# Bank reads first, tiles half a pair apart, and a fixed TensorE order in the second pass of a two-layer graph kernel

## The chip, the cores and the metric

The kernel runs on one NeuronCore of one Trainium2 chip. The metric is the device time of one execution in microseconds (us). The kernel before takes 2579.47 us, the median of three runs that lie between 2577.24 and 2579.74 us. The profiled execution spans 2577.0 us; every time that is read from the trace counts from its start.

Five engines run beside each other, each with a queue of its own: TensorE (PE in the profile; its weight loads are shown apart as PEld), VectorE (DVE), ScalarE (ACT), GpSimd (POOL) and the DMA-issuing SyncE (SP).

## The reference

There are 128 graphs of 64 nodes with 768 features. Two layers of a graph network run one after the other. Only the second one is touched here:

```python
def _L1_gnn_ref(feat_in, adj, W, b, w_src, w_dst, H_w, H_b):
    h = jnp.einsum('bni,hio->bhno', feat_in, W)          # 6 heads of 128
    th = jnp.tanh(h)
    attn_src = jnp.einsum('bhno,hoz->bhnz', th, w_src)
    attn_dst = jnp.einsum('bhno,hoz->bhnz', th, w_dst)
    attn = attn_src + jnp.swapaxes(attn_dst, -1, -2)
    attn = jnp.where(attn >= 0, attn, leaky_alpha * attn)
    attn = jnp.where((adj == 0)[:, None, :, :], NEG_MASK, attn)
    attn = jax.nn.softmax(attn, axis=-1)
    feat_out = jnp.einsum('bhnm,bhmo->bhno', attn, h) + b
    feat_out = jax.nn.elu(...)                           # heads side by side: 768 columns
    gate = jax.nn.sigmoid(feat_in @ H_w.T + H_b)
    return gate * feat_out + (1.0 - gate) * feat_in

x = x + _L0_gnn_ref(relu(layernorm(x)), ...)             # pass 1 of the kernel
x = x + _L1_gnn_ref(relu(layernorm(x)), ...)             # pass 2 of the kernel
```

So each row of 768 features is multiplied by two 768 x 768 matrices (`W`, all heads, and `H_w`), and a small attention inside each graph of 64 nodes follows.

## The kernel before

Two graphs make a tile of 128 rows, and two tiles (`t0`, `t1`) make a pair; there are 32 pairs. Pass 2 multiplies the 256 rows of a pair by both matrices at once with a bilinear scheme of 15 products of blocks in place of 18. `f...` are sums of transposed blocks of the input, `g...` and `b...` sums of weight blocks, and each product is added in one of four PSUM banks a, b, c and d. After each product VectorE (and, where an output block begins, ScalarE too) reads the bank and adds it to an output block of the tile.

```python
PRODUCTS = (      # A side, B side, bank, bank starts anew, output block (tile, third), sign, ...
    ("f1", "g6", "a", True, "11", "+", False),
    ("f7", "g10", "b", True, "00", "-", False),
    ("a01", "b11", "d", True, "01", "+", True),
    ("f4", "b21", "a", False, "01", "-", False),
    ("a00", "g12", "b", False, "01", "-", False),
    ("f3", "g8", "c", True, "12", "-", False),
    ("a02", "g14", "a", False, "00", "-", False),
    ("f9", "g9", "b", False, "02", "+", False),
    ("f11", "b10", "d", True, "00", "+", True),
    ("f6", "g5", "a", False, "02", "+", False),
    ("f8", "g3", "b", False, "12", "-", False),
    ("f10", "b12", "c", False, "02", "+", True),
    ("f5", "b22", "a", False, "12", "-", False),
    ("a11", "g1", "b", False, "11", "+", True),
    ("f2", "g11", "a", False, "10", "+", True),
)
```

`P1` to `P15` below are these products in this order. The code of pass 2, cut to what the change and the steps of the prediction touch:

```python
psm = px.enter_context(tc.tile_pool(name="psm1", bufs=2, space=bass.MemoryType.PSUM))
pss = px.enter_context(tc.tile_pool(name="pss1", bufs=2, space=bass.MemoryType.PSUM))  # two buffers "ps"

def merged(main, side):              # writes the side steps between the numbered main steps
    side = sorted(side, key=lambda e: e[0])
    ...
def turn(p, k, q):                   # transposes two blocks of the next pair's input   (L704)
    ps = pss.tile([P, 512], F32, name="ps")...
    for i in range(KQ):
        nc.tensor.transpose(ps[:, i, :], H1[2 * p + k][...], ident)
    a = OPS[p, f"a{k}{q}"] = ...
    nc.scalar.copy(a, ps)                                                  # (L709)

def read(b, c, sign, first, ss):     # after a product
    ...
    op = nc.vector.tensor_add if sign == "+" else nc.vector.tensor_sub
    if not first:
        ... op(to, ps, to) or op(to, to, ps)                               # (L736, L738)
        return
    if ss.start == 0:
        nc.scalar.activation(to[:, 0], ps[:, 0], AF.Copy, ...)             # (L741)
    if ss.stop == 2:
        ... op(to[:, s], ps[:, s], hbb[:, cols])                           # (L746, L748)

def product(an, bn, b, first, c, sign, begins, ss):
    def step(q):                     # two steps (q = 0, 1) a product
        if first and q == 0:
            bank[b] = psm.tile([P, 512], F32, name=f"pm{b}", bufs=2 if b == "a" else 1)
        nc.tensor.matmul(bank[b][...], OPS[p, an][:, q, :], bw2[bn][...], ...)   # (L755)
        if q == KQ - 1:
            read(b, c, sign, begins, ss)

def heads(t):                        # tanh, products with w_src and w_dst, sums by head
    th = work.tile([P, H, DO], F32, name="th")
    nc.scalar.activation(th, HS[t], AF.Tanh)                               # (L774)
    pr = work.tile([P, 2, H, DO], F32, name="pr")
    nc.vector.tensor_mul(pr, th..., wsd...)                                # (L776)
    for h in range(H):               # 12 activations with an accumulator  (L781, L783)
        nc.scalar.activation(pr[:, 1, h, :], pr[:, 1, h, :], AF.Copy, accum_out=sd[:, 1, h : h + 1])
    ...                              # then a short chain on GpSimd into sdb (L784 to L791)

def rows(t):                         # (L803): PE, then DVE into rrow (L805) and ACT into lrow (L807)
    ps = pss.tile([P, 512], F32, name="ps")
    nc.tensor.matmul(ps[:NR, : N + P], sdb[t % 2]..., idr, start=True, stop=True)
    ...
def gate(t):
    nc.scalar.activation(Z[t], Z[t], AF.Tanh, scale=0.5)                   # (L811)

def softmax(t):
    pl = pss.tile([P, 512], F32, name="ps")...
    nc.tensor.matmul(pl, lrow[t % 2], rrow[t % 2], start=True, stop=True)  # (L819)
    nc.vector.copy_predicated(a, AI[p]..., pl)                             # (L821)
    nc.scalar.activation(al, a, AF.Prelu, alpha=LEAKY)                     # (L823)
    nc.vector.tensor_reduce(mx, al, AX.X, OP.max, negate=True)             # (L825)
    for h in range(H):                                                     # six exponentials (L829)
        nc.scalar.activation(pb[:, h, :], al[:, h, :], AF.Exp, bias=mx[:, h : h + 1],
                             accum_out=dn[:, h : h + 1])
    nc.vector.reciprocal(dn, dn)

def turn_p(t):                       # three transposes of the probabilities (L840), two heads in each
    ps = pss.tile([P, 512], F32, name="ps")...
    for c in range(HH):
        nc.tensor.transpose(ps[:, c, :], PB[t][:, 2 * c : 2 * c + 2, :]..., ident)
    nc.scalar.copy(pt, ps)                                                 # (L842)

def attend(t):                       # 12 small matmuls (L857), then six reads by VectorE (L861)
    po = [pss.tile([P, 512], F32, name="ps")... for r in range(2)]
    ...
def final(t, c0=0, c1=D):            # ACT exponential (L871), three DVE operations (L872 to L874), out
    ...
```

`before(p)` transposes the next pair's blocks, `own(p)` forms sums and calls `heads(t0)`, `behind(p)` holds the rest of the attention of the pair before. Nothing in the source fixes the order on an engine: a scheduler takes the instructions of all engines and orders each engine's queue by priority (earlier in the source first) as its own model finds them ready. What is fixed in the built program is that each engine takes its queue in that order.

Of the kernel before, what the change touches and what calls it, by code (L numbers as in the profile page):

```python
# [8 lines left out]
F32 = mybir.dt.float32  # L9
# [70 lines left out]
def kernel(  # L80
# [558 lines left out]
    with ExitStack() as px:  # L639
# [78 lines left out]
        def main(p):  # L718
# [2 lines left out]
            steps = []  # L721
            for k in range(2):
                t = 2 * p + k
                HS[t] = hzs[t % 4][:, 0, :].rearrange("p (h o) -> p h o", h=H)
                Z[t] = hzs[t % 4][:, 1, :]

            def read(b, c, sign, first, ss):

                k, q = int(c[0]), int(c[1])
                cols = slice(q * CQ, (q + 1) * CQ)  # L730
                to = hzs[(2 * p + k) % 4][:, ss, cols]
                ps = bank[b][:, : (ss.stop - ss.start) * CQ].rearrange("p (s n) -> p s n", n=CQ)
                op = nc.vector.tensor_add if sign == "+" else nc.vector.tensor_sub
                if not first:
                    if sign == "+":
                        op(to, ps, to)  # L736
                    else:
                        op(to, to, ps)  # L738
                    return
                if ss.start == 0:  # L740
                    nc.scalar.activation(to[:, 0], ps[:, 0], AF.Copy,  # L741
                                         scale=1.0 if sign == "+" else -1.0)
                if ss.stop == 2:
                    s = 1 - ss.start
                    if sign == "+":
                        op(to[:, s], ps[:, s], hbb[:, cols])  # L746
                    else:
                        op(to[:, s], hbb[:, cols], ps[:, s])  # L748

            def product(an, bn, b, first, c, sign, begins, ss):  # L750
                def step(q):
                    if first and q == 0:
                        bank[b] = psm.tile([P, 512], F32, name=f"pm{b}", bufs=2 if b == "a" else 1)
                    n = ss.stop - ss.start
                    nc.tensor.matmul(  # L755
                        bank[b][:, : n * CQ], OPS[p, an][:, q, :],
                        bw2[bn][:, (2 * q + ss.start) * CQ : (2 * q + ss.stop) * CQ],
                        start=(first and q == 0), stop=(q == KQ - 1), skip_group_check=True)
# [159 lines left out]

        def last():


            p = NP - 1
            t0, t1 = 2 * p, 2 * p + 1
            return [(31, lambda: (heads(t1), swap(t1))),
                    (31, lambda: load_x(t0)),
                    (33, lambda: load_x(t1)),
                    (38, lambda: rows(t0)),
                    (40, lambda: softmax(t0)),
                    (46, lambda: rows(t1)),
                    (48, lambda: softmax(t1)),  # L930
                    (54, lambda: turn_p(t0)),
                    (56, lambda: attend(t0)),
                    (99, lambda: gate(t0)),
                    (99, lambda: gate(t1)),
                    (99, lambda: turn_p(t1)),
# [58 lines left out]
```

## Time and profile before

| | |
|---|---|
| device time, median of 3 | 2579.47 us |
| span of the profiled execution | 2577.0 us |
| PE busy | 2489.3 us (97%) |
| DVE busy | 1980.3 us (77%) |
| ACT busy | 1079.5 us (42%) |
| first transpose of pass 2 on PE | 1513.72 us |
| first product of the last pair | 2513.76 us |
| last matmul of the attention | 2562.4 us |

"PE" counts the matmul records; "PEld" counts the weight loads, which run beside matmuls. In a list of instructions in order of time each row has a start, a duration, the engine, the line of the source, what is written from what, and how often; a bracket at the end of a row tells how long the engine stood idle before it and which instruction ended the wait. A product of two matmuls of 128 x 512 shows as four records of line 755.

### The profile page before, as it was taken

To read this page: it belongs to the slowest core of one execution; us is meant where nothing else is said; L and a number is where in the kernel's file an instruction comes from. 1 tells how busy PE (TensorE), PEld (TensorE's weight loads), DVE (VectorE), ACT (ScalarE), POOL (GpSimd) and SP (SyncE) were. 2 spreads that over 40 slices of the span, in tenths; PEclk is the share of its full clock that TensorE was granted. 3 is DMA by queue.
4 is the path that set the end of the run, shared out by engine and by line. 5 is a ranking of instruction groups with operands and counts; after the bars stand their busy time and mean duration, and the time that the engine had idled before them with its cause. 6 is when DMAs were issued, how large, how long until landed. Compare 5 with 4: busy or idle time off the path is not lost.

```text
span 2577.0 us, 35545 instructions
## 1 busy us (share of the span) xinstructions
PE 2489.3 (97%) x12072; PEld 1714.2 (67%) x12072; DVE 1980.3 (77%) x4130; ACT 1079.5 (42%) x3588; POOL 492.3 (19%) x801
## 2 busy tenths in 40 slices
PE   5999999999999999999999999999999999999996
PEld 4788888888888888888888864444444444444444
DVE  8977777777777777777777557888888888888887
ACT  1222222222222122222222216666666666666666
POOL 0121121211212112121121111222222222222222
PEclk8999999999999999999999999999999999999998
DMA  5122121221312212122121263444444444444433
GB/s 172 56 74 80 52 102 52 76 78 52 103 52 76 78 52 102 52 78 76 52 101 50 79 203 78 100 100 100 99 100 100 101 100 101 99 100 100 100 75 77
DMA packets 115047, 224.19 MB, mean 87 GB/s; under 512 B 36538, under 2 KB 48941, under 8 KB 114866
## 3 DMA queue, kind: packets, MB, share of 16 engines
q1 hardware_dynamic: 105208, 196.70, 23.3%
q0 software_dynamic: 9504, 25.17, 6.9%
q8 instruction: 95, 1.56, 0.3%
q14 instruction: 86, 0.70, 0.1%
q10 hardware_dynamic: 154, 0.06, 0.0%
HBM read 95.67 MB, written 100.66 MB: 76 GB/s over the span
## 4 chain that ended last, share of the span: by engine, by line
PE 71%; DVE 18%; ACT 6%; issue 4%; DMA 1%; POOL 1%; SPq 0%; POOLq 0%; DVEq 0%; ACTq 0%
PE pwa L544 19%; PE pwb L544 16%; PE pwc L544 6%; PE pma L755 6%; PE pwd L544 6%; PE pmb L755 6%; PE pb L497 5%; DVE f L861 3%; ACT pb L829 3%; DVE op L243 3%; PE pmc L755 2%; DVE pr L776 2%; DVE f L874 2%; DVE f L872 2%; DVE weights L738 1%
## 5 line engine op out<-in xcount | busy, mean ns | idle before, releaser
L544 PE MATMUL pwa<-weights,op 128*128 128x256 f32 x2304 | 542.6, 383 | 4.3 <-DVE x L536 3.1
L544 PEld LDWEIGHTS pwa<-weights,op 128*128 128x128 f32 x2304 | 423.0, 190 | 73.4 <-DVE x L536 12.0
L243 DVE TENSOR_TENSOR op<-op 128x768 f32<-128x768 f32 (+1 forms) x512 | 339.8, 683 | 156.4 <-ACT op L505 154.5
L505 ACT COPY op<-pb 128x768 f32<-128x768 f32 x160 | 124.2, 798 | 757.0 <-PE pb L497 757.0
L755 PE MATMUL pma<-weights,op 128*128 128x512 f32 (+1 forms) x792 | 381.5, 597 | 35.2 <-DVE weights L738 29.3
L544 PE MATMUL pwb<-weights,op 128*128 128x256 f32 x1536 | 372.2, 383 | 12.9 <-DVE x L538 9.5
L544 PEld LDWEIGHTS pwb<-weights,op 128*128 128x128 f32 x1536 | 285.9, 191 | 60.7 <-DVE x L538 10.3
L755 PE MATMUL pmb<-weights,op 128*128 128x512 f32 (+1 forms) x528 | 252.4, 591 | 3.6 <-DVE weights L738 3.5
L755 PEld LDWEIGHTS pma<-weights,op 128*128 128x128 f32 x792 | 137.8, 191 | 173.8 <-issue 96.4
L225 POOL TENSOR_TENSOR rn<-ve,mhalf 128x1 f32<-128x1 f32 x128 | 89.0, 695 | 530.5 <-DVE ve L224 526.9
L544 PE MATMUL pwc<-weights,op 128*128 128x256 f32 x768 | 184.9, 383 | 0.0
L544 PE MATMUL pwd<-weights,op 128*128 128x256 f32 x768 | 176.2, 379 | 0.0
L755 PEld LDWEIGHTS pmb<-weights,op 128*128 128x128 f32 x528 | 97.0, 193 | 118.4 <-issue 82.9
L218 DVE BATCH_NORM_STATS2 st<-x 128x6 f32<-128x384 f32 x256 | 136.4, 547 | 44.7 <-DMA x<-in_x_dram 43.5
L476 POOL COPY c<-cnt 128x243 bf16<-128x243 bf16 x64 | 46.2, 751 | 649.3 <-PE pb L484 602.3
L497 PE MATMUL pb<-r,h 64*128 64x192 f32 x1536 | 153.0, 339 | 7.8 <-ACT h L406 7.7
L544 PEld LDWEIGHTS pwc<-weights,op 128*128 128x128 f32 x768 | 143.2, 190 | 25.1 <-issue 7.0
L544 PEld LDWEIGHTS pwd<-weights,op 128*128 128x128 f32 x768 | 145.9, 190 | 19.8
L572 ACT ACTIVATE hf<-x,rn 128x768 f32<-128x768 f32 x64 | 65.8, 1028 | 213.7 <-DVE rn L226 213.7
L497 PEld LDWEIGHTS pb<-r,h 64*128 64x128 f32 x1536 | 124.6, 189 | 42.7 <-issue 30.5
L829 ACT ACTIVATE pb<-al,mx 128x64 f32<-128x64 f32 x384 | 128.3, 335 | 14.8 <-DVE mx L825 14.8
L574 POOL TENSOR_TENSOR x<-x,hf 128x768 f32<-128x768 f32 x64 | 115.9, 1812 | 85.4 <-ACT hf L572 85.4
(152 smaller groups left out, 4160.3 us busy)
## 6 DMA issues: line engine op xcount, KB each, us to landing
x<-in_x_dram SPq DMA_DIRECT2D x64, 384.0 KB
h<-hf SPq DMA_DIRECT2D x64, 384.0 KB
out_dram<-x SPq DMA_DIRECT2D x64, 384.0 KB
hh<-hh SPq DMA_DIRECT2D x64, 384.0 KB
h<-h SPq DMA_DIRECT2D x64, 384.0 KB
x<-hh SPq DMA_DIRECT2D x64, 384.0 KB
hx<-weights SPq DMA_DIRECT2D x128, 192.0 KB
out_dram<-f POOLq DMA_DIRECT2D x62, 384.0 KB, 4.9
```

The source lines that it names most:

```text
L218: ins = nc.vector.bn_stats(st[:, i, :], src[:, i * HALF : (i + 1) * HALF])
L225: nc.gpsimd.tensor_tensor(to[:, 0:1], ve, mhalf, op=OP.pow)
L243: return (nc.vector.tensor_add if s1 == "+" else nc.vector.tensor_sub)(to, x, y)
L497: nc.tensor.matmul(ps[:, g, i * 3 * N : (i + 1) * 3 * N], H0[t][s, kb * P : (kb + 1) * P], rts[p % 2][s, k].rearrange("p s n -> p (s n)"), ...
L505: nc.scalar.copy(a.rearrange("p h s (g n) -> p g (h s) n", g=GT), ps[:, :, : 6 * N].rearrange("p g (x n) -> p g x n", n=N))
L544: nc.tensor.matmul(bank[b][:, :CQ], OPS[p, an][:, q, s, :], bw[bn][:, (s * KQ + q) * CQ : (s * KQ + q + 1) * CQ], start=(first and q == s ...
L572: nc.scalar.activation(h, X[t], AF.Relu, scale=to[:, 0:1], bias=to[:, 1:2])
L574: nc.gpsimd.tensor_add(X[t], X[t], h)
L755: nc.tensor.matmul(bank[b][:, : n * CQ], OPS[p, an][:, q, :], bw2[bn][:, (2 * q + ss.start) * CQ : (2 * q + ss.stop) * CQ], start=(first a ...
L776: nc.vector.tensor_mul(pr, th[:, None].to_broadcast([P, 2, H, DO]), wsd.rearrange("p s (h o) -> p s h o", h=H))
L829: nc.scalar.activation(pb[:, h, :], al[:, h, :], AF.Exp, bias=mx[:, h : h + 1], accum_out=dn[:, h : h + 1])
L861: nc.vector.scalar_tensor_tensor(FF[t][:, h * DO : (h + 1) * DO], po[h % 2][:, h // 2, :], DN[t][:, h : h + 1], bb, op0=OP.mult, op1=OP.add)
```

## The change

Pass 1 stays as it is. In pass 2 four things change:

- **Bank reads take precedence.** The reads of a product's bank are put in with a high priority, so the scheduler places them ahead of other work that is ready on VectorE and ScalarE. They are to free a bank as soon as its product is done.
- **The two tiles of a pair run half a pair apart.** The attention of `t0` stays one pair behind; the attention of `t1` starts half a pair later, and its `turn_p`, `attend` and `final` fall two pairs behind (`behind2`). This is to spread the attention work over the pair.
- **Six places for the outputs.** A tile's outputs (`HS`, `Z`) live longer so, and get six places in place of four; the two new ones are tiles of their own. To make room, `pr` has one buffer in place of two.
- **TensorE keeps the written order.** `manual_schedule` for PE takes the order of the PE queue from the source; the four other queues are still ordered by the scheduler.

```diff
+    NHZ = 6
...
+        hzs += [wb.tile([P, 2, D], F32, name=f"hz{i}") for i in range(4, NHZ)]
...
-                HS[t] = hzs[t % 4][:, 0, :].rearrange("p (h o) -> p h o", h=H)
-                Z[t] = hzs[t % 4][:, 1, :]
+                HS[t] = hzs[t % NHZ][:, 0, :].rearrange("p (h o) -> p h o", h=H)
+                Z[t] = hzs[t % NHZ][:, 1, :]
...
                     if q == KQ - 1:
-                        read(b, c, sign, begins, ss)
+                        with tc.high_priority():
+                            read(b, c, sign, begins, ss)
...
-            pr = work.tile([P, 2, H, DO], F32, name="pr")
+            pr = work.tile([P, 2, H, DO], F32, name="pr", bufs=1)
...
         def behind(p):
...
-            return [(0, lambda: gate(t0)),
-                    (1, lambda: (heads(t1), swap(t1))),
-                    (2, lambda: load_x(t0)),
-                    (4, lambda: gate(t1)),
-                    (4, lambda: rows(t0)),
-                    (6, lambda: softmax(t0)),
-                    (10, lambda: load_x(t1)),
-                    (11, lambda: rows(t1)),
-                    (13, lambda: softmax(t1)),
-                    (12, lambda: turn_p(t0)),
-                    (14, lambda: attend(t0)),
-                    (15, lambda: final(t0)),
-                    (19, lambda: turn_p(t1)),
-                    (21, lambda: attend(t1)),
-                    (22, lambda: final(t1))]
+            return [(1, lambda: gate(t0)),
+                    (7, lambda: rows(t0)),
+                    (9, lambda: softmax(t0)),
+                    (9, lambda: (heads(t1), swap(t1))),
+                    (10, lambda: load_x(t0)),
+                    (14, lambda: gate(t1)),
+                    (17, lambda: turn_p(t0)),
+                    (19, lambda: attend(t0)),
+                    (20, lambda: final(t0)),
+                    (22, lambda: rows(t1)),
+                    (24, lambda: softmax(t1)),
+                    (25, lambda: load_x(t1))]
+
+        def behind2(p):
...
+            return [(2, lambda: turn_p(t1)),
+                    (4, lambda: attend(t1)),
+                    (5, lambda: final(t1))]
...
         # last(): the steps of the last pair, moved later and joined by turn_p, attend and
         # final of the tile before (cut)
...
+        px.enter_context(tc.manual_schedule(engines={mybir.EngineType.PE}))
         for _, step in before(0):
             step()
         for p in range(NP):
-            more = [(3, lambda: finish(NP - 1))] if p == 0 else []
+            more = behind(p - 1) + behind2(p - 2)
+            if p == 0:
+                more.append((3, lambda: finish(NP - 1)))
             if p == NP - 1:
-                more += last()
-            merged(main(p), own(p) + before(p + 1) + behind(p - 1) + more)
+                more = [(1.3 * i, f) for i, f in more] + last()
+            merged(main(p), own(p) + before(p + 1) + more)
```

More of the change, by code (lines that the diff above doesn't have):

```diff
@@ L730, in read @@
                 cols = slice(q * CQ, (q + 1) * CQ)
-                to = hzs[(2 * p + k) % 4][:, ss, cols]
+                to = hzs[(2 * p + k) % NHZ][:, ss, cols]
                 ps = bank[b][:, : (ss.stop - ss.start) * CQ].rearrange("p (s n) -> p s n", n=CQ)
@@ L902, in behind @@
             t0, t1 = 2 * p, 2 * p + 1
-            return [(0, lambda: gate(t0)),
-                    (1, lambda: (heads(t1), swap(t1))),
-                    (2, lambda: load_x(t0)),
-                    (4, lambda: gate(t1)),
-                    (4, lambda: rows(t0)),
-                    (6, lambda: softmax(t0)),
-                    (10, lambda: load_x(t1)),
-                    (11, lambda: rows(t1)),
-                    (13, lambda: softmax(t1)),
-                    (12, lambda: turn_p(t0)),
-                    (14, lambda: attend(t0)),
-                    (15, lambda: final(t0)),
-                    (19, lambda: turn_p(t1)),
-                    (21, lambda: attend(t1)),
-                    (22, lambda: final(t1))]
+            return [(1, lambda: gate(t0)),
[11 more added lines that the diff above has]
+        def behind2(p):
+            if p < 0:
+                return []
+            t1 = 2 * p + 1
+            return [(2, lambda: turn_p(t1)),
+                    (4, lambda: attend(t1)),
+                    (5, lambda: final(t1))]
         def last():
@@ L923, in last @@
             t0, t1 = 2 * p, 2 * p + 1
[L924 to L932, printed above, removed]
+            tl = t0 - 1
+            tl = t0 - 1
+            return [(32, lambda: (heads(t1), swap(t1))),
+                    (34, lambda: load_x(t0)),
+                    (36, lambda: load_x(t1)),
+                    (46, lambda: rows(t0)),
+                    (47, lambda: turn_p(tl)),
+                    (49, lambda: softmax(t0)),
+                    (50, lambda: attend(tl)),
+                    (51, lambda: final(tl)),
+                    (54, lambda: rows(t1)),
+                    (57, lambda: softmax(t1)),
+                    (99, lambda: turn_p(t0)),
+                    (99, lambda: attend(t0)),
                     (99, lambda: gate(t0)),
```

## The prediction

> **What bounds the kernel now.** I read the busy shares of the page, then its slices, then the waits of TensorE in pass 2, then one pair in order of time.
>
> ```profile
> span 2577.0 us, 35545 instructions
> PE 2489.3 (97%) x12072; PEld 1714.2 (67%) x12072; DVE 1980.3 (77%) x4130; ACT 1079.5 (42%) x3588; POOL 492.3 (19%) x801
> PE   5999999999999999999999999999999999999996
> ```
>
> TensorE is busy almost throughout. Whatever changes the time must shorten or lengthen its queue. Its waits between 1600 and 2500 us, all of them but one of 0.3 us:
>
> ```profile
> PE pma L755 <- DVE weights L738: 28.5, 28, 1.0
> ```
>
> One wait of 1.0 us in each pair. PE and VectorE in order of time show where, and then ScalarE's durations:
>
> ```profile
> 1934.40 1.88 PE L755 MATMUL pmd<-weights,op 128*128 128x512 f32 x4
> 1937.29 1.13 PE L755 MATMUL pma<-weights,op 128*128 128x512 f32 x2 [1.02 <-DVE weights L738]
> ...
> 1935.35 0.95 DVE L874 SCALAR_TENSOR_TENSOR f<-weights,f 128x768 f32<-128x768 f32 x1
> 1936.22 0.42 DVE L243 TENSOR_TENSOR op<-op 128x256 f32<-128x256 f32 x1
> 1936.56 0.68 DVE L738 TENSOR_TENSOR weights<-weights,pma 128x512 f32<-128x512 f32 x1
> ...
> 1918.02 0.33 ACT L829 ACTIVATE pb<-al,mx 128x64 f32<-128x64 f32 x1
> 1918.35 0.33 ACT L829 ACTIVATE pb<-al,mx 128x64 f32<-128x64 f32 x1
> 1919.88 0.46 ACT L842 COPY pT<-ps 128x384 f32<-128x384 f32 x1
> 1936.64 0.36 ACT L741 ACTIVATE weights<-pma 128x256 f32<-128x256 f32 x1
> 1936.91 0.37 ACT L741 ACTIVATE weights<-pmd 128x256 f32<-128x256 f32 x1
> ```
>
> P15 may not write bank a before P13's read has emptied it, and VectorE does that read only after elementwise work (L874, L243). The product before began at 1934.40 and takes 1.72 us, so PE loses 1937.29 - 1934.40 - 1.72 = 1.17 us. The pair lasts 1937.29 - 1905.04 = 32.25 us, in which the table of stretches gives PE 31.23, DVE 26.57 and ACT 22.51 us of work. So the best that any reordering can bring here is 1.17 us in each of about 30 pairs: 35 us, 1.4%.
>
> **What the Trainium skill says.** "PSUM — Partial Sum Buffer", section "Engine vs sequencer instructions": the queues of ScalarE, VectorE and GpSimdE are strict first-in first-out, and matmuls start and finish in program order. The trace agrees: the 0.68 us read stood 1.2 us behind the elementwise work while PE waited for it. So the order in which a queue was built is the order in which it runs, and a ready instruction behind one that waits does not pass it. "Perfetto Trace Analysis", section "Tensor Engine Instruction (MATMUL, LD_WEIGHTS)": a matmul's end in the profile is estimated. Here a product's records end 0.16 us after the next product starts (1.88 against 1.72), and a ScalarE read starts 0.04 us after that end (1907.02 to 1907.06); I use 0.20 us from a product's nominal end to a reader's start.
>
> **The change, part by part.** No arithmetic is added or removed: a pair still has 15 products, 12 + 6 transposes, 24 attention matmuls. What decides is the order of the queues, which can be read in the built program. It is the same in each of the pairs numbered 2 to 30 (29 pairs) on PE, DVE and ACT; pass 1 is unchanged. On PE around the pair's start it is P15, P1, three transposes of `turn_p(t1)`, P2, `attend(t1)`, P3. ScalarE's order there:
>
> ```
> tanh (heads); gate; Prelu of t1's softmax; 2 accumulations; read of P15; 1 accumulation;
> 4 exponentials of t1; READ OF P1; 2 exponentials of t1; 7 accumulations; READ OF P2;
> 2 accumulations; COPY OF pT (t1); ...
> ```
>
> The bank reads have gone in front of attention work that PE needs *before or right after* the very product they wait for. Four waits follow, each from the start spacing of ScalarE instructions above: a read 0.27, an exponential 0.33, an accumulation 0.29 (L781, 1933.43 to 1933.72), pT 0.47, hand-over to PE 0.08 (pT ends 1920.34, PE starts 1920.42), a transpose 0.11, an input copy 0.25 started, 0.37 whole.
>
> 1. Transposes of `turn_p(t1)`. The last two exponentials run only after the read of P1, and the third transpose needs them: 0.20 + 0.27 + 0.66 + 0.15 (accumulator read and hand-over) = 1.28 us after P1's end, then 0.11 for itself. Unhindered, all three take 0.33. Loss 1.28 + 0.11 - 0.33 = 1.06 us at the least.
> 2. `attend(t1)` needs pT, which stands behind the read of P2 and two accumulations: 0.20 + 0.27 + 0.58 + 0.47 + 0.08 = 1.60 us after P2's end. Nothing stands between P2 and attend on PE. Loss 1.6 us.
> 3. `attend(t0)` now follows four input transposes directly, and there are only two "ps" buffers, so it needs both input copies. They can start 0.42 us after the first transpose (1925.28 to 1925.70) and the second ends at about 1.05; with the hand-over the second attention matmul starts at 1.09, where the transposes end at 0.44. Loss 0.6 us.
> 4. In P12 two pairs of input transposes stand together. The second reuses the "ps" buffer of `rows(t1)`, which ScalarE frees with lrow (0.26 us) queued behind the copy of the first pair: 0.42 + 0.26 + 0.26 + 0.04 = 0.98, where PE would go on at 0.22. Loss 0.76 us.
>
> Sum 4.0 us. Against it stands the wait that goes: the read of P13 now has only one elementwise operation of 0.95 us ahead of it and P14's 1.72 us to run in, so 1.17 us is gained. Net +2.8 us a pair as a floor. I also walked the three queues through one whole pair with these durations. There the exponentials come another 0.2 us late (the max waits behind the 1.68 us product of `heads`, L776), `rows(t0)` waits 0.35 us for VectorE to free its buffer, and `softmax(t0)` waits 0.33 us for lrow, which stands behind the 0.94 us exponential of `final`. That makes 4.9 us of waits, +3.7 net. Small pauses of PE, some 0.1 us after attention matmuls, will swallow part of the last two. I take the middle, +3.3 us: a pair of 35.5 us.
>
> 29 x 3.3 = 96 us. Pair 1 has half of it: +1. In the last pair PE now waits, in the profile before, 2.48 + 3.55 + 0.78 + 1.14 us; the new order puts products into those holes but more attention of the tile before into this pair: -2. Together 2579.5 + 96 + 1 - 2 = 2674 us.
>
> **The rivals.**
>
> *A. The reads win what they aim at.* The 1.17 us wait goes and the attention waits are hidden: 2579 - 35 = 2544, with a tighter last pair perhaps 2535. For it: DVE (26.6) and ACT (22.5) have room in 32 us, and spreading t0 and t1 removes a crowd. Against it: waits 1 and 2 do not depend on how busy ScalarE is, since its queue waits for a product that PE has just finished.
>
> *B. The time stays within 2%.* For this the four losses would have to add up to under 3 us in place of 4 to 4.9, so that less than 1.8 us a pair is left after the gain. One of the two large waits would have to be half as long, by a ScalarE that passes data on faster than the rows above show, or the transposes and attention would have to find other buffers than I read in the build. Against it: the durations come from the same instructions. Then 2590 to 2630.
>
> *C. Worse than the sum.* A late `turn_p` delays everything ScalarE does next (pT, tanh of t1, the product of `heads`, the sums for `rows`), and these come back as a later `rows` and `softmax`, a loop around the pair that I closed with the soft waits of 0.35 and 0.33 only. If it opens further, +5 us a pair: 2725.
>
> **Range and chances.** The floor of the four waits gives 2579 + 29 x 2.8 = 2660, the walk 2579 + 29 x 3.7 = 2687, and either way a few us for the last pair. Widened by a hand-over misjudged by 0.2 us at each of four places (0.8 x 29 = 23 us): 2640 to 2705. The 2% mark lies at 2631, that is +1.8 us a pair; the two large waits alone (2.66 - 1.17 = 1.5) stay below it, and with both small ones they pass it clearly. Faster by over 2% would take 52 us, more than all of PE's waits: 0.02. Within 2% 0.10, slower 0.88.
>
> **What would show it.** In the profile after, PE's waits in pass 2 should name ScalarE: about 1.1 us in each pair for pb (exponentials) before the transposes of `turn_p`, about 1.6 us for pT before attend, 0.6 and 0.76 us for input copies and lrow; the wait for VectorE's read of P13 should be gone; PE's work a pair should stay at 31.2 us and the pair last 35.5. ScalarE should stand idle for a PE product just ahead of those exponentials and of pT. I am wrong if the pair takes 31 to 32 us, or if PE's waits name VectorE or a DMA, or if the loss lies at the end of the kernel rather than in every pair.

## The result, and the profile after

The changed kernel takes 2672.57 us (median of four runs, 2671.89 to 2674.03). The kernel before took 2578.56 us beside it. The ratio is 1.0365, with a 95% interval of 1.0348 to 1.0383: 3.65% slower, 94 us. The prediction said 2674.

The page of the kernel after, its span, busy times and TensorE's slices:

```profile
span 2670.9 us, 35403 instructions
PE 2506.5 (94%) x12072; PEld 1731.6 (65%) x12072; DVE 2009.1 (75%) x4130; ACT 1079.1 (40%) x3588; POOL 487.1 (18%) x801
PE   6999999999999999999999998989899898988995
```

The matmuls are the same 12072, and TensorE's share falls from 97% to 94%. Pass 1 (the nines on the left) is untouched; in pass 2 the nines are now mixed with eights. So most of the time was lost in waits, spread evenly over pass 2. The waits of TensorE between 1600 and 2590 us name them; the columns after the colon are us in total, how often, and the longest:

```profile
PE ps L860 <- ACT pT L845: 39.7, 28, 1.4
PE ps L843 <- ACT pb L832: 25.9, 56, 0.6
PE ps L706 <- ACT op L711: 13.0, 28, 0.5
PE ps L822 <- ACT lrow L810: 7.1, 28, 0.5
PE ps L860 <- ACT op L711: 6.8, 28, 0.2
PE ps L806 <- DVE f L864: 4.6, 28, 0.2
```

Before, there was one wait in each pair, for VectorE's read of P13. It is gone. Six others stand in its place, and five of them name ScalarE: for pT ahead of `attend` (L860), for the exponentials ahead of `turn_p` (L843), for the input copies (L711), for lrow (L810).

The two largest are seen in TensorE's list in order of time. The idle time in brackets is shorter than the loss, since a record runs on for a while after the next instruction could have started (1.88 us for a product that takes 1.72); I read the losses from start to start.

```profile
2000.71 0.27 PE L843 MATMUL ps<-ident,pb 128*128 128x128 f32 x1
2001.31 0.33 PE L843 MATMUL ps<-ident,pb 128*128 128x128 f32 x1 [0.33 <-ACT pb L832]
2002.24 0.33 PE L843 MATMUL ps<-ident,pb 128*128 128x128 f32 x1 [0.60 <-ACT pb L832]
2002.40 1.88 PE L757 MATMUL pmb<-weights,op 128*128 128x512 f32 x4
2005.71 0.32 PE L860 MATMUL ps<-weights,pT 64*64 64x128 f32 x1 [1.42 <-ACT pT L845]
```

The three transposes take 2002.40 - 2000.71 = 1.69 us in place of 0.33. P2 starts at 2002.40, and after its 1.72 us TensorE has nothing to do until pT is there: 2005.71 - 2004.12 = 1.59 us.

ScalarE at the same time (L832 exponentials, L743 bank reads, L786 accumulations, L845 the copy pT), and below it VectorE a little earlier (L779 the product of `heads(t0)`, L828 the max of the softmax of t1, without which no exponential can start):

```profile
2000.83 0.34 ACT L832 ACTIVATE pb<-al,mx 128x64 f32<-128x64 f32 x1
2001.16 0.36 ACT L743 ACTIVATE hz<-pma 128x256 f32<-128x256 f32 x1
2001.42 0.34 ACT L832 ACTIVATE pb<-al,mx 128x64 f32<-128x64 f32 x1
...
2003.83 0.30 ACT L786 ACTIVATE pr<-pr 128x128 f32<-128x128 f32 x1
...
2004.32 0.38 ACT L743 ACTIVATE hz<-pmb 128x256 f32<-128x256 f32 x1
...
2004.90 0.30 ACT L786 ACTIVATE pr<-pr 128x128 f32<-128x128 f32 x1
2005.19 0.47 ACT L845 COPY pT<-ps 128x384 f32<-128x384 f32 x1
...
1996.84 1.74 DVE L779 TENSOR_TENSOR pr<-th,wsd 128x1536 f32<-128x1536 f32 x1
1999.10 0.54 DVE L828 TENSOR_REDUCE mx<-al 128x6 f32<-128x384 f32 x1
```

The read of P1 stands between the fourth and the fifth exponential. The read of P2 starts 0.20 us after P2's end, two accumulations and pT follow. That is the predicted chain. But ScalarE hardly stood idle ahead of either read (no gap ahead of the first, some 0.2 us ahead of the second). From the first exponential on it had work of its own to do almost all the time. And the exponentials started late, only 0.88 us before P1 ended (1999.83 to 2000.71), because the max stood on VectorE behind the 1.74 us product. This matters below.

The last pair, two of TensorE's longest waits there:

```profile
2641.26 0.34 PE L822 MATMUL ps<-rrow,lrow 82*128 82x384 bf16 x1 [2.77 <-ACT lrow L810]
...
2654.86 0.52 PE L843 MATMUL ps<-ident,pb 128*128 128x128 f32 x3 [2.22 <-DVE f L864]
```

Where the 93.9 us between the two profiles lie:

| | before | after | difference |
|---|---|---|---|
| up to the first product of the last pair | 2513.76 us | 2598.66 us | +84.9 |
| last pair and tail | 63.2 us | 72.2 us | +9.0 |
| for comparison: one pair in mid-pass | 32.25 us | 35.27 us | +3.02 |

29 such pairs make +87.6 us; what lies ahead of them gives back 84.9 - 87.6 = -2.7 us.

### The profile page after: what moved, and what is told of

Its sections match the earlier page's. It is cut to its first block, busy times and chain, and to the rows that moved or that the text cites. A ratio compares the mean times of both kernels' runs of the same rounds, so it can differ in the third digit from the quotient of the medians.

```text
span 2670.9 us, 35403 instructions
## 1 busy us (share of the span) xinstructions
PE 2506.5 (94%) x12072; PEld 1731.6 (65%) x12072; DVE 2009.1 (75%) x4130; ACT 1079.1 (40%) x3588; POOL 487.1 (18%) x801
## 4 chain that ended last, share of the span: by engine, by line
PE 75%; ACT 9%; DVE 6%; issue 4%; POOL 3%; DMA 2%; SPq 0%; POOLq 0%; ACTq 0%; DVEq 0%
PE pwa L545 18%; PE pwb L545 15%; PE pwc L545 6%; PE pma L757 6%; PE pmb L757 6%; PE pwd L545 6%; PE pb L498 5%; PE pmc L757 4%; ACT pr L784 3%; ACT pb L832 2%; POOL sdb L792 2%; PE pmd L757 2%; DVE pr L779 2%; PE ps L706 1%; PE ps L860 1%
## 5 line engine op out<-in xcount | busy, mean ns | idle before, releaser
L757 PE MATMUL pma<-weights,op 128*128 128x512 f32 (+1 forms) x792 | 372.7, 586 | 2.3 <-DVE weights L748 1.5
L757 PEld LDWEIGHTS pma<-weights,op 128*128 128x128 f32 x792 | 145.0, 191 | 154.2 <-issue 149.0
L779 DVE TENSOR_TENSOR pr<-th,wsd 128x1536 f32<-128x1536 f32 x64 | 112.0, 1751 | 42.8 <-ACT th L777 42.8
L784 ACT ACTIVATE pr<-pr 128x128 f32<-128x128 f32 x384 | 113.8, 298 | 74.2 <-DVE pr L779 40.5
```

The costliest lines, as they stand in the source:

```text
L757: nc.tensor.matmul(bank[b][:, : n * CQ], OPS[p, an][:, q, :], bw2[bn][:, (2 * q + ss.start) * CQ : (2 * q + ss.stop) * CQ], start=(first a ...
```

## The experiments

The change has three parts that can be set apart: bank reads first, the half-pair distance with its six places, and the fixed order of TensorE. My theory (Q in the expectations) was the prediction's: the reads of P1 and P2, put in front of attention work on ScalarE, make the two large waits. The rival (F): the fixed order is to blame, which lets TensorE do nothing else while it waits. A third (S): the longer distance of t1 and its six places cost.

**e1: after without precedence for the reads.**

```diff
-                        with tc.high_priority():
-                            read(b, c, sign, begins, ss)
+                        read(b, c, sign, begins, ss)
```

> The changed kernel without the high priority of the bank reads; all else stays. Theory Q (ScalarE's queue order: reads that wait for a product stand ahead of attention work that TensorE needs): ScalarE now has all six exponentials ahead of the reads of P15 and P1, and the pT copy ahead of the read of P2, so TensorE's waits for pb (0.9 us a pair) and pT (1.4) go. But VectorE now has the product of heads, the max and a sum ahead of the read of P13, so P15 waits again for VectorE, some 1.8 us. Together about 34.3 us a pair, 2635 to 2655 us. Rival F (the fixed TensorE order is what costs): no change, 2672 within 6 us. Rival S (the longer distance of t1 and six output places cost): no change either.

Measured: 2640.39 us, ratio 1.0232 (1.0215 to 1.0249), a pair of 34.23 us. As expected. The two largest waits of TensorE, 1600 to 2500 us:

```profile
PE pma L757 <- DVE weights L740: 25.8, 17, 1.5
PE pma L757 <- DVE hz L740: 13.7, 9, 1.5
```

These two rows, 26 pairs together, are the wait for P13's read, back again and longer than before, since VectorE's 1.7 us product of `heads` now stands in front of that read too. The waits for pb and pT are gone. Precedence thus costs 32 us here, and the kernel is still 60 us slower than before: two thirds of the loss lie elsewhere.

**e2: after, with `attend(t1)` and `final(t1)` one product later.**

```diff
-                    (4, lambda: attend(t1)),
-                    (5, lambda: final(t1))]
+                    (6, lambda: attend(t1)),
+                    (7, lambda: final(t1))]
```

> The changed kernel with attend(t1) one product later (behind P3 and not behind P2); the read of P2 still stands ahead of the pT copy on ScalarE. Theory Q: pT is ready 1.6 us after P2's end, P3 takes 1.72 us, so the wait for pT goes and nothing else changes: -1.4 to -1.6 us a pair, 33.8 us, 2622 to 2634 us in all. Rival F: the order is as fixed as before, 2672. Rival S: 2672.

Measured: 2705.43 us, ratio 1.048 (1.0464 to 1.0495), pairs of 35.30 and 36.88. A miss, and in the wrong direction. The wait for pT went as expected. The largest wait of TensorE, and then one of its places in TensorE's list and VectorE's:

```profile
PE ps L806 <- DVE f L864: 52.2, 25, 2.1
```

```profile
1983.39 0.25 PE L806 MATMUL ps<-idr,sdb 128*82 128x192 bf16 x1 [2.09 <-DVE f L864]
...
1979.86 1.76 DVE L779 TENSOR_TENSOR pr<-th,wsd 128x1536 f32<-128x1536 f32 x1 [1.27 <-ACT th L777]
...
1981.87 1.64 DVE L864 SCALAR_TENSOR_TENSOR f<-ps,dn,bb 128x128 f32<-128x128 f32 x6
```

`rows(t0)` now comes half a product after `attend(t1)`. It needs a "ps" buffer that `attend` has filled, and VectorE empties it only behind the product of `heads`. A wait of 1.59 us was moved and became one of 2.35 us (1983.39 - 1981.04, with half of P4 starting at 1980.18 and taking 0.86).

That alone costs nothing: 11 of the 29 pairs take some 35.3 us, as in after. The other 18 take 36.88, and they are just those in which TensorE's granted clock (1.00 is the full one) fell to half for 3.41 us. Two pairs, one of each kind (columns: us, then busy time and count of PE, PEld, DVE, ACT and POOL, granted clock, DMA share, GB/s):

```profile
1896.81:1932.11 35.30, 31.58 (x132) 14.55 (x130) 27.43 (x55) 22.61 (x97) 7.24 (x16) 1.00 0.40 93
1932.11:1968.99 36.88, 33.16 (x132) 15.20 (x130) 27.58 (x55) 22.60 (x97) 6.60 (x16) 0.95 0.37 87
```

18 x 1.58 = 28 of the 33 us by which e2 is slower than after are the clock's. What halves it is not shown here: in the pair above the slow stretch begins right behind the wait of `rows`, yet the same wait stands in the pairs without one.

**e3: after with three "ps" buffers.**

```diff
-        pss = px.enter_context(tc.tile_pool(name="pss1", bufs=2, ...))
+        pss = px.enter_context(tc.tile_pool(name="pss1", bufs=3, ...))
```

> The changed kernel with three ps buffers in PSUM for two. Theory Q: the waits for input copies before attend(t0), 0.6, in P12, 0.76, and before rows, 0.16, go. The build also changes ScalarE's order: the exponentials of t1 now come ahead of the read of P1, so the wait for pb falls from 1.36 to some 0.3; pT now stands behind the read of P2 and five accumulations (two before), so its wait grows from 1.5 to 2.4. Net -1.7 us a pair: 33.6 us, 2615 to 2635 us. Rival (the two buffers are not what those two waits are about): waits on ScalarE before the input transposes and attend(t0) stay, and only the other two move, 2665 to 2675.

Measured: 2640.51 us, ratio 1.0232 (1.0217 to 1.0247), a pair of 34.1: some 5 us above the range. Waits 3 and 4 of the prediction, for input copies, are gone with a third buffer. But the scheduler also built the queues of ScalarE and VectorE anew: the exponentials came in front of the read of P1, five accumulations in front of pT, and the max in front of the product of `heads`. So the wait for pb went too, and that for pT grew. TensorE's largest wait, then VectorE and the first exponential:

```profile
PE ps L860 <- ACT pT L845: 61.2, 26, 2.4
...
1950.89 0.54 DVE L828 TENSOR_REDUCE mx<-al 128x6 f32<-128x384 f32 x1
1951.35 1.75 DVE L779 TENSOR_TENSOR pr<-th,wsd 128x1536 f32<-128x1536 f32 x1
...
1951.46 0.35 ACT L832 ACTIVATE pb<-al,mx 128x64 f32<-128x64 f32 x1 [2.01 <-DVE mx L828]
```

The exponentials now start 2.05 us before P1 ends (at 1953.51) in place of 0.88.

**e4: after with a free order of TensorE.**

```diff
-        px.enter_context(tc.manual_schedule(engines={mybir.EngineType.PE}))
```

> The changed kernel without the fixed TensorE order: the scheduler orders TensorE as in the kernel before; priority of reads, half-pair distance and six places stay. Rival F: the loss goes with it, 2580 or less. Theory Q: the fixed order costs only because it puts turn_p and attend right next to the products that ScalarE waits for; in the build the scheduler now puts P3 and P4 between P2 and attend(t1), so pT, behind the read of P3, is ready 1.3 us after P3 and its wait goes; in every second pair five exponentials still stand behind the read of P1, but four products stand ahead of turn_p there. So most of the loss goes here too, 2570 to 2620 us, and TensorE's remaining waits name VectorE or ScalarE in single places.

Measured: 2553.83 us, ratio 0.9898 (0.9884 to 0.9913), pairs of 31.55 and 31.2 us in turn. One line less makes the kernel 119 us faster, and faster than before. With the reads still first, all of the loss goes when TensorE's order is given back to the scheduler. That is what rival F forecast (2580 or less). Theory Q also expected most of the loss to go, but its range of 2570 to 2620 is missed by 16 us.

**e5 and e6: the kernel before with one part alone**, precedence (e5) and fixed order (e6).

```diff
-                        read(b, c, sign, begins, ss)
+                        with tc.high_priority():
+                            read(b, c, sign, begins, ss)
```

> The kernel before with one part of the change alone: the high priority of the bank reads. TensorE's order is the scheduler's, four places, tiles as before. Theory: the priority does what it is for. In the build VectorE reads P13 right after attend's six reads and before the product of heads, P15 stands after P14 again, and TensorE's wait of 1.17 us a pair goes; ScalarE's copies of pT and the exponentials have products enough between them and TensorE's use. 31.2 to 31.6 us a pair, 2545 to 2560 us. Rival (the priority is what costs, whoever orders TensorE): waits for pb or pT appear, over 2600 us.

```diff
+        px.enter_context(tc.manual_schedule(engines={mybir.EngineType.PE}))
         for _, step in before(0):
```

> The kernel before with one part of the change alone: TensorE keeps the written order. No priority, four places, positions of before. Theory (a fixed order costs where the written places put work right behind what it depends on): softmax(t0) is written one product after rows(t0), but its lrow stands on ScalarE behind the read of P2 and twelve accumulations that wait for the product of heads; TensorE waits there some 3 us a pair, and 1 us or so for the reads of P2 and P13. 34 to 35.5 us a pair, 2630 to 2680 us. Rival (only the priority of the reads makes the fixed order costly): 2580 within 15 us.

e5 measured: 2595.14 us, ratio 1.0058 (1.0041 to 1.0074), 35 us above the range. P13's wait went, and TensorE's waits, then its place, GpSimd and VectorE show what came:

```profile
PE ps L804 <- POOL sdb L790: 40.0, 27, 2.3
```

```profile
1985.56 0.28 PE L804 MATMUL ps<-idr,sdb 128*82 128x192 bf16 x1 [1.36 <-POOL sdb L790]
...
1982.91 1.62 POOL L792 TENSOR_TENSOR sg<-sg,sdb 128x18 f32<-128x18 f32 x1
1984.87 0.22 POOL L792 TENSOR_TENSOR sg<-sg,sdb 128x18 f32<-128x18 f32 x1
...
1982.68 1.77 DVE L777 TENSOR_TENSOR pr<-th,wsd 128x1536 f32<-128x1536 f32 x1
```

`rows` waits for the short chain on GpSimd. One operation of that chain took 1.62 us where its twin took 0.22, just while VectorE ran its 1.77 us product of `heads`. The surplus of 1.40 us is as long as the wait of 1.36 in this pair. The Trainium skill, "GPSIMD Engine Reference", section "1. Specifications", says that GpSimd shares its ports to the on-chip memory with VectorE and is held up by VectorE's instructions with two inputs from there; the lines agree. So does the rest of the trace: between 1600 and 2480 us all 24 of these operations that start inside a product of `heads` take 1.61 or 1.62 us, while the median of the others is 0.22. No run here tests it alone.

e6 measured: 2747.56 us, ratio 1.0655 (1.0639 to 1.0671), a pair of 37.26. The direction was expected, the size was 68 us above the range. The two largest waits of TensorE, and VectorE around one of the first kind:

```profile
PE pma L755 <- DVE weights L738: 64.2, 24, 2.7
PE ps L819 <- ACT lrow L807: 40.3, 24, 2.2
```

```profile
1993.25 0.95 DVE L874 SCALAR_TENSOR_TENSOR f<-weights,f 128x768 f32<-128x768 f32 x1
1994.12 1.75 DVE L776 TENSOR_TENSOR pr<-th,wsd 128x1536 f32<-128x1536 f32 x1
...
1996.46 0.68 DVE L738 TENSOR_TENSOR weights<-weights,pma 128x512 f32<-128x512 f32 x1
```

P13 ended at 1992.65; its read starts at 1996.46, behind 0.95 and 1.75 us of elementwise work and two short sums. The same wait as before, 2.7 us long in place of 1.0, where some 1 us was expected; the wait for lrow, expected at 3 us, was 2.2 at most. 13 of the 29 pairs have stretches of half clock here too; they take 37.93 us in the mean and the others 37.26, which makes some 9 of the 169 us.

**e7: fixed order kept, but fitted.** Precedence for VectorE's reads only, three "ps" buffers, and `turn_p`, `attend`, `final` of t1 spaced out.

```diff
-        pss = px.enter_context(tc.tile_pool(name="pss1", bufs=2, ...))
+        pss = px.enter_context(tc.tile_pool(name="pss1", bufs=3, ...))
...                      # high priority put around the two vector operations of read() alone
-            return [(2, lambda: turn_p(t1)),
-                    (4, lambda: attend(t1)),
-                    (5, lambda: final(t1))]
+            return [(4, lambda: turn_p(t1)),
+                    (8, lambda: attend(t1)),
+                    (9, lambda: final(t1))]
```

> The changed kernel, TensorE still in the written order, with each of the four waits taken away: ScalarE's bank reads without priority (VectorE's keep it), three ps buffers, turn_p(t1) and attend(t1) two products later. Theory Q: none of the waits for pb, pT, input copies and lrow is left; 31.3 to 32.2 us a pair, 2550 to 2580 us. Rival F (a fixed order costs whatever is in it): 2630 or more.

Measured: 2591.77 us, ratio 1.005 (1.0035 to 1.0065), a pair of 32.69, 12 us above the range. The two largest waits:

```profile
PE ps L823 <- ACT lrow L811: 25.3, 28, 1.2
PE pma L759 <- DVE weights L750: 14.2, 19, 0.8
```

The waits for pb, pT and input copies are gone, which brings 81 us of the 94 with TensorE's order still fixed; that for lrow, which the expectation had as gone too, is left. So rival F fails in its strict form: what costs is not that an order is fixed, but what the order is together with the other queues. e7 changes three things at once and does not tell what each is worth.

**e8: before with precedence and three "ps" buffers**, the edits of e5 and e3 together.

> The kernel before with the priority of the reads and a third ps buffer, TensorE's order by the scheduler. Theory: TensorE is left without waits, as in the run with the priority alone; the third buffer adds little: 31.2 to 31.5 us a pair, 2543 to 2558 us. Rival: with more buffers the scheduler bunches the input transposes and new waits for ScalarE's copies appear, 2570 to 2600 us.

Measured: 2637.93 us, ratio 1.0225 (1.0208 to 1.0241). A miss by 80 us, and 38 us above the rival's range: with a buffer more it is 43 us slower than e5. The wait for GpSimd stayed (52.1 us in 26 waits) and one for input copies came (10.7). The larger part is again the clock: 16 of the 29 pairs have a stretch of half clock and take 34.92 us, the others 33.2, and 16 x 1.70 makes 27 of the 43 us. In e5 one pair has such a stretch.

**e9: after, where only ScalarE's reads of P1 and P2 lose precedence.** This is the sharpest test of the prediction's cause for its waits 1 and 2; everything else, TensorE's order too, stays.

```diff
...                      # high priority put around the two vector operations of read(), as in e7
-                    nc.scalar.activation(to[:, 0], ps[:, 0], AF.Copy,
-                                         scale=1.0 if sign == "+" else -1.0)
+                    with (ExitStack() if c in ('00', '11') else tc.high_priority()):
+                        nc.scalar.activation(to[:, 0], ps[:, 0], AF.Copy,
+                                             scale=1.0 if sign == "+" else -1.0)
```

> The changed kernel, TensorE in the written order; only ScalarE's reads of P1 and P2 lose their priority, all other reads keep it. The build has the six exponentials ahead of the read of P1 and the pT copy ahead of the read of P2; TensorE's order is the same and VectorE's nearly. Theory Q as the prediction put it (TensorE waits because those two reads stand ahead): both waits go, -2.9 us a pair, 32.4 us, 2580 to 2600 us. Theory Q2 (turn_p and attend stand too close behind softmax(t1): ScalarE has a tanh, a gate, three accumulations, the six exponentials and nine accumulations to do in that stretch whatever the order): the third exponential pair is ready about 1.1 us after P1, pT about 4.5 us after P1 and so 1.5 us after P2; waits of 0.9 and 1.5 us stay, 34.6 to 35.0 us a pair, 2650 to 2668 us.

Measured: 2670.39 us, ratio 1.0354 (1.0337 to 1.0371): no different from after. ScalarE's queue was changed as intended:

```
after: read P15, 1 accumulation, 4 exp, READ P1, 2 exp, 7 accumulations, READ P2, 2 accumulations, pT
e9:    read P15, 1 accumulation, 6 exp, 9 accumulations, READ P1, pT, READ P2
```

and TensorE still waits:

```profile
2003.61 0.33 PE L845 MATMUL ps<-ident,pb 128*128 128x128 f32 x1 [0.33 <-ACT pb L834]
...
2006.86 0.32 PE L862 MATMUL ps<-weights,pT 64*64 64x128 f32 x1 [1.21 <-ACT pT L847]
...
2011.54 0.25 PE L808 MATMUL ps<-idr,sdb 128*82 128x192 bf16 x1 [0.92 <-DVE f L866]
```

From start to start, `turn_p(t1)` loses 1.09 us (after: 1.36), `attend(t1)` 1.37 (after: 1.59), and `rows(t0)` 1.08 (after: 0.33). Taking the reads away brings 0.27 and 0.22 us, about one read each, and the next consumer loses it again. The rest is ScalarE's other work: six exponentials of 0.33 us that start as late as in after, 0.88 us before P1 ends (2001.47 to 2002.35), since the max stands behind the product of `heads` here too; and nine accumulations of 0.29 us ahead of pT. (The read of P1 still stands ahead of pT, but P1 has long ended by then.) The first theory falls.

**e10, e11, e12: the free order, refined.** e10 is after without fixed order and without precedence (the edits of e4 and e1). e11 is e4 with ScalarE's read of P2 alone without precedence. e12 is e4 with ScalarE's reads of P1 and P2 without precedence and three "ps" buffers.

> The changed kernel without the fixed TensorE order and without the priority of the reads: half-pair distance and six places are left. If the distance alone brings the gain of the free-order run (2554), it stays: the build puts P15 behind P1 and half of P3, 4.5 us after P13, which is time enough for VectorE's read of P13, 31.2 to 31.7 us a pair, 2548 to 2570 us. If the priority is needed for it, P15 waits for the read of P13 as in the kernel before, 32.2 us, 2572 to 2590 us.

> Free TensorE order, priority of the reads but for ScalarE's read of P2, half-pair distance, six places. In the build every pair has one and the same order; exponentials end 1.1 us after P15, P1 in between; pT is ready 0.8 us before attend(t1), which stands behind P4. No wait on TensorE: 31.2 us in every pair (the free-order run alternates 31.55 and 31.2), 2542 to 2553 us. Rival: another wait appears (VectorE's read of P2 comes only 1 us before P5 needs the bank): 2560 or more.

> As the run before, with ScalarE's read of P1 without priority too and a third ps buffer. The waits that the free-order run has left (0.3 us for pb, 0.5 for lrow in every second pair) may go with it: 31.2 us a pair, 2542 to 2553 us. Rival: the buffer lets the scheduler bunch input transposes and rows, as in the kernel before with priority and three buffers, and new waits come: 2565 or more.

Measured: e10 2535.54 us, ratio 0.9834 (0.9819 to 0.9849); e11 2556.58, ratio 0.9915 (0.99 to 0.9929); e12 2553.26, ratio 0.9902 (0.9888 to 0.9917). e10 is faster than both kernels and than expected. e11 and e12 lie 3.6 and 0.3 us above their ranges, and nothing was won over e4; in e12 GpSimd's chain became a wait (21.8 us in 15). The largest wait of e10 between 1600 and 2500 us:

```profile
PE ps L821 <- ACT lrow L809: 6.8, 29, 0.3
```

One wait of 0.2 us in each pair is left, beside four single ones of 2.9 us together, and this is reached without precedence for any read. With a free order the scheduler put six matmul records of products (one and a half products) between the second and the third transpose of `turn_p(t1)` and six more ahead of `attend(t1)`, so that TensorE has products to do while ScalarE works.

**The three parts together.** All with two "ps" buffers:

| half-pair distance, six places | reads first | TensorE's order fixed | us |
|---|---|---|---|
| no | no | no | 2578.56 (before) |
| no | yes | no | 2595.14 (e5) |
| no | no | yes | 2747.56 (e6) |
| yes | no | no | 2535.54 (e10) |
| yes | yes | no | 2553.83 (e4) |
| yes | no | yes | 2640.39 (e1) |
| yes | yes | yes | 2672.57 (after) |

The kernel before took 2578.4 to 2580.2 us beside these runs, so the rows can be compared to some 2 us. Fixing the order costs 169 us alone, 105 with the distance, 119 with distance and precedence. Precedence costs 17 to 32 us in each of its three places. The distance with its six places gains 43 us alone, 41 beside precedence and 107 under a fixed order. So rival S fails, and the change is one good part and two bad ones. Not tried: reads first and fixed order without the distance; whether four places would do as well for the distance; what one buffer for `pr` and the new steps of the last pair, which go with the distance in these rows, cost or bring.

## Why the prediction was right, and where it was wrong

**The size and the four waits: right.** The losses in one pair, from start to start in TensorE's list:

| | predicted, floor or walk | measured |
|---|---|---|
| 1 `turn_p(t1)` | 1.06; walk 1.26 | 1.36 |
| 2 `attend(t1)` | 1.6 | 1.59 |
| 3 `attend(t0)` | 0.6 | 0.57 |
| 4 second transposes in P12 | 0.76 | 0.63 |
| `rows(t0)` | walk 0.35 | 0.33 |
| `softmax(t0)` | walk 0.33 | 0.40 |
| sum | 4.0; walk 4.9 | 4.88 |

The walk through the three queues was right to 0.15 us in every term. The method holds: take the built order of each queue, take each duration from a start spacing in the trace before, and let each queue run strictly in order. This rests on what the Trainium skill says under "PSUM — Partial Sum Buffer", section "Engine vs sequencer instructions": strict queues on ScalarE, VectorE and GpSimd, and matmuls in program order. The lists of TensorE and ScalarE after run in the very order that the prediction read in the build.

**The gain: right.** P13's read no longer holds up P15. PE and VectorE after, in order of time:

```profile
1995.56 1.88 PE L757 MATMUL pmb<-weights,oq 128*128 128x512 f32 x4
1997.28 3.17 PE L757 MATMUL pma<-weights,op 128*128 128x512 f32 x7
...
1994.67 0.94 DVE L877 SCALAR_TENSOR_TENSOR f<-weights,f 128x768 f32<-128x768 f32 x1
1995.76 0.69 DVE L740 TENSOR_TENSOR weights<-weights,pma 128x512 f32<-128x512 f32 x1
```

The read starts at 1995.76, behind one operation of 0.94 us, and P15 starts at 1997.28, exactly 1.72 us after P14.

**The pair: 35.27 us for 35.5.** Net +3.02 where +3.3 was taken and the walk had +3.7. Waits of 4.88 less the 1.17 gained make +3.71; the rest of the pair became 0.69 us shorter (32.25 - 1.17 = 31.08 before, 35.27 - 4.88 = 30.39 after), which I put down to small pauses. The prediction allowed for such pauses and took 0.4.

**The last pair: wrong.** "The new order puts products into those holes but more attention of the tile before into this pair: -2." It became 9.0 us longer. With a fixed order TensorE meets `rows`, `softmax` and `turn_p` one after the other with few products between, and waits 1.0 to 2.8 us at seven places; its bracketed waits there add to 17.1 us, 8.7 before. This offset the pairs, which came out lower (29 x 3.02 = 87.6 in place of 96): 87.6 - 2.7 + 9.0 = 93.9. That the total of 2674 us was met to 1.5 us is luck: two errors of some 10 us cancelled.

**The cause named for waits 1 and 2: wrong.** "The bank reads have gone in front of attention work that PE needs before or right after the very product they wait for." The order is as described, the sum of that chain fits to 0.01 us for `attend`, and yet these two reads were hardly the cause: e9 takes both out of the way and wins 2 us. The failed step is the argument against rival A, that these waits "do not depend on how busy ScalarE is". They do. The sign that the prediction asked for, a ScalarE idle for a product just ahead of that work, is hardly there: in after it is idle for 1.18 us before its accumulations, but for VectorE's product of `heads`.

What the traces show in its place differs for the two waits.

- Wait 1, `turn_p(t1)`: four products (P13 to P1) stand between `softmax(t1)` and it, and yet the exponentials come late, because the max of the softmax, which they need, is late on VectorE. e9 and e3 both have all exponentials ahead of the read of P1 and the same TensorE order there. In e9 the max stands behind the product of `heads` and the exponentials start 0.88 us before P1 ends; TensorE waits. In e3 it stands ahead and they start 2.05 us before; the wait is gone. In e1 it stands behind, but without precedence the reads of P13 and P14 no longer hold up VectorE ahead of it: counted from the start of P13, the first exponential comes at 4.36 us, in after at 5.99. By this, precedence costs here through VectorE's reads rather than ScalarE's; but no run moves the max alone, so it stays argued.
- Wait 2, `attend(t1)`: one product stands between `turn_p(t1)` and it, while ScalarE has accumulations to do ahead of pT. e2 and e7 (a later place) and e4 and e10 (a free order) remove the wait. In e1 it is gone as well, but there TensorE has stood 1.68 us for P13's read before P15; pT is ready only 0.2 us before `attend(t1)` needs it.

**The limit of a reordering: wrong.** "The best that any reordering can bring here is 1.17 us in each of about 30 pairs: 35 us." e10 brought 43. The stretch of one pair in e10 (columns as under e2), with one pair of after below:

```profile
1943.91:1974.66 30.75, 30.52 (x132) 14.27 (x131) 26.84 (x55) 22.25 (x97) 6.50 (x16) 1.00 0.49 107
...
1960.30:1995.56 35.26, 31.81 (x132) 14.65 (x130) 27.57 (x55) 22.46 (x97) 7.22 (x16) 1.00 0.39 91
```

TensorE's busy time for the same work was 31.23 before, is 31.81 in after and 30.52 in e10. It is not a measure of work, since a record runs on into the pause behind it. (The Trainium skill, "Perfetto Trace Analysis", section "Tensor Engine Instruction (MATMUL, LD_WEIGHTS)", says that the ends of matmul records are estimated.) Counted from start to start, the work of a pair divides so (the counts are of records):

| us in one pair | before | after | e10 |
|---|---|---|---|
| 60 of products | 27.97 | 28.34 | 26.65 |
| 12 of input transposes | 1.34 | 2.39 | 1.31 |
| 6 of `turn_p` | 0.72 | 2.02 | 0.65 |
| 48 of `attend` | 1.69 | 2.00 | 1.62 |
| `rows`, `softmax` | 0.53 | 0.51 | 0.52 |
| sum | 32.25 | 35.26 | 30.75 |

Each row holds the pauses behind its instructions. Twelve records of products back to back take 5.16 us in after, 0.43 each, so 60 need 25.80. Before, they took 2.17 us more: the wait of 1.17 and 1.0 of small pauses that no bracket shows and that I had counted as work. e10 wins 1.32 us in this row and 0.18 in the others, 1.50 in all and 29 x 1.50 = 43.5: the wait and 0.33 us of such pauses. Its products still lie 0.85 us above 25.80.

## What to carry to other kernels

Read the built order of every queue and walk it with start spacings from the trace: that gave the time of a reordering to some 0.15 us a term. But a wait that a chain explains to the last 0.01 us need not be caused by the link you suspect: take that link out before you name it the cause, for an engine with other work to do fills the place, and the link that counts may lie a queue further back (here VectorE's max ahead of ScalarE's exponentials). Before an in-order engine's sequence is fixed by hand, leave as much of its own work between a producer on another engine and its consumer as that producer's whole queue needs; here the free order with the half-pair distance alone (2535.54 us) beat everything that was forced. And look at the granted clock of single pairs before a slower run is put down to its waits.

## What was not expected of the hardware

A GpSimd operation on 128 x 18 elements took 1.62 us in e5 in place of 0.22 while VectorE ran a product of 1.77 us over two inputs, enough by its size to make the wait of `rows` there. In after, 25 such small operations that started inside a product of `heads` took 1.64 to 1.72 us. TensorE's records hid 1.0 us of pauses in a pair of 32 us. And TensorE's granted clock fell to half for 3.41 us at a time, in 18 of 29 pairs in e2, 16 in e8 and 13 in e6, and in none in before and after; in e2 and e8 it made the pair 1.6 to 1.7 us longer.
